# Putting a sparse graph layer's hand-ordered stage under the list scheduler, with a third early slot for 12 tiles and edge lists built in the message loop

## The chip, the cores and the metric

The kernel runs on one core of a Trainium2 chip. The metric is the device time of one execution in microseconds (us). Before the change three runs took 649.17, 649.49 and 644.71 us; their median, 649.17 us, is the time before.

## The reference

Four graph layers follow one another on the same 2708 nodes with 128 features. All use one sparse adjacency matrix `adj` (2708 x 2708; an entry is present with probability 0.003, so a row has some 8, and a row's present entries all have the value 1 divided by their number). Each layer adds to `x` a function of `h`, the rectified layer norm of `x`. `NORM`, `LOG`, `EXP` and `H_ADD` stand for the row norm, and for the hyperbolic logarithm, exponential and addition, each of which needs a few sums per row and a factor per row.

```python
# layer 0
h = max(layernorm(x), 0)
e = H_ADD(EXP(LOG(h) @ embed), embed_bias)
neigh = EXP(adj @ LOG(e))
x = x + H_ADD(EXP(LOG(concat(h, neigh)) @ layer), layer_bias)
# layer 1
h = max(layernorm(x), 0)
s, d = h @ msg_w[:, :D].T, h @ msg_w[:, D:].T
agg[i] = sum_j adj[i, j] * gelu(s[i] + d[j] + msg_b)
new = concat(h, agg) @ upd_w.T + upd_b
x = x + layernorm(gelu(new) + h) * ln_w + ln_b
# layer 2
h = max(layernorm(x), 0);  x = x + max(adj @ (h @ w2), 0)
# layer 3
h = max(layernorm(x), 0);  x = x + h @ w_self + (adj @ h / clip(rowsum(adj), 1)) @ w_neigh
```

The gelu of layer 1 stands inside the sum over edges, so the rows `d[j]` have to be fetched for every edge; the other layers use the matrix as a mask in plain products.

## The kernel before

**Tiling.** The nodes make T = 22 tiles of 128 rows (the last has 20 rows). Four tiles make a block, so there are six blocks, the last of two tiles. Blocks 0 to 2 (tiles 0 to 11) are the first half, blocks 3 to 5 (tiles 12 to 21) the second. The work of `sparse_stack` falls into a beginning, the sparse stage of layer 0, the message loop of layer 1, and layers 2 and 3. A flag that tells whether the matrix fits the kernel's lists is worked out beside it; if it is set, `dense_stack` computes everything again.

**The sparse stage of layer 0** (lines 818 to 1542) is written in order and lets the framework order the engines, apart from a few places where `queue_behind` holds an operation until another one has been issued.

- The rows of the embedding are scaled (line 1465) and cut into three bf16 parts (`split`, line 797). ACT and DVE turn the adjacency matrix, read by columns, into an fp8 mask (line 992). PE multiplies parts with mask, one product for each of the six blocks of columns (line 1284, 66 matmuls a block).
- For each block PE also packs the mask into words (line 1021). From these DVE finds which columns of a row are present (`find_words`, `find_columns`) and lays them out in slots (`lay_out`, `ext` at line 1130): two early slots, four head slots, and the rest of the edges in a tail of up to three lists of 128 edges a tile. `pack_edges` (line 1204) builds the tail's lists for a block of tiles: two DVE operations a tile (lines 1214 and 1217), three small matmuls a tile (line 1227), an ACT copy (line 1235) and some dozen DVE operations.
- `neighbours` (line 1316) and `update` (line 1357) finish layer 0 for one half: norms and factors, own rows (line 1342), new `x` (line 1368), normalised rows on ACT (line 920), their transposes on PE (line 930), the products `d` (line 941), and the writes of `d` to two tables in HBM: `d_hbm` for all nodes and `d_early` for the first half alone (line 1389). For the first half the transposes are held until three quarters of block 4's product have been issued.
- `gather_early` (line 1483) has POOL fetch the rows for the two early slots from `d_early`. This is 44 indirect DMAs of 128 rows. It can start when the first half's `d` is written, before the second half is finished. Columns of the second half that stand in an early slot are moved to the tail.

**The message loop of layer 1** (lines 1720 to 2195) is ordered by a list scheduler in the program itself. `op` records an operation with its engine, an assumed duration, what it follows and a due time; `carry_out` (line 1588) works through them in assumed time and issues them in that order, which then is the fixed order of each engine's queue. `ring` counts buffers: the operation waits until the one that many places earlier has been freed.

- `prelude` (line 1736) computes, for one block, the rows `s` and the rows' own part of the update, and cuts `s` into three parts.
- `messages` (line 1801) does one tile. POOL gathers the head slots and then the tail from `d_hbm`; both have four buffers. DVE adds `s`, ACT applies gelu, PE sums over the slots and multiplies by the update weights.
- `update` (line 1945) ends two tiles. `share` (line 2105) adds a tile's rows to the product of layer 2, and `check_half` (line 2136) compares the adjacency rows of 13 tiles with the found value in two halves of 1354 columns. Both are fillers, taken where an engine has nothing due.

```python
        g4 = op("POOL", 5.08, begin_head, gathered[-1:], when - 10.2, ring=("g", 4))
        g3 = op("POOL", 1.27 * nq, begin_tail, [g4], when - 5.1, ring=("gt", 4))
```

Each gather is one indirect DMA, so a full tile has seven in the loop, four for the head and three for the tail; all tiles together have 88 and 64. Layers 2 and 3 follow, ordered by the same scheduler; the change touches there only the sum over the checks' counts.

## Time and profile before

| what | before |
| --- | --- |
| median of the runs | 649.17 us |
| profiled execution, own time | 653.21 us |
| its span | 651.4 us |
| busy PE, DVE, ACT, POOL | 430.5, 412.4, 321.0, 224.0 us |
| gathers of the loop: head, tail | 88 of 1028 ns, 64 of 1008 ns |
| first product matmul (line 1284) | at 62.0 us |
| first and last early gather (line 1487) | at 169.4 and 226.2 us |
| first and last gather of the loop (line 1810) | at 272.8 and 511.3 us |
| last tile's new row in the loop (line 1890) | at 544.7 us |

The profile is of one execution. Times are counted from its first instruction; the span is from the first to the last one, and the execution's own time has a little around it. POOL is the engine that issues the gathers. [...] "Remote" or "another core or an unknown queue" as releaser of a wait means that the profile shows no event that ended it. Each engine works through its queue in order, so an operation that waits holds everything behind it.

### The profile page before, as it was taken

How to read it: one execution, taken by the hardware profiler on the slowest of the kernel's cores; microseconds unless marked ns; L12 is line 12 of the kernel's file. 1: busy time of each engine (PE TensorE's matmuls, PEld its weight loads, DVE VectorE, ACT ScalarE, POOL GpSimd, SP SyncE). 2: the span in 40 equal slices, each digit the busy share in tenths (PEclk: the TensorE clock that was granted, in tenths of full speed). 3: DMA queues.
4: the chain of work that ended last, by engine and by line, in shares of the span. 5: the costliest groups of instructions: out<-in, count | busy, mean ns of one | idle time of the engine just before them, and what ended most of it. 6: DMA issues, size and time to landing. Idle time of an engine off the chain costs nothing.

```text
span 651.4 us, 8164 instructions
## 1 busy us (share of the span) xinstructions
PE 430.5 (66%) x2467; PEld 295.6 (45%) x2467; DVE 412.4 (63%) x1715; ACT 321.0 (49%) x634; POOL 224.0 (34%) x277
## 2 busy tenths in 40 slices
PE   2956999999930003632177777837577888899875
PEld 2642444756720002532064544534445544678764
DVE  6879596578832166642155654565567648799963
ACT  3788677714200122321043533746567662899821
POOL 8500000000477700277465655665676300000000
PEclk9987999799955555666558987967799889999979
DMA  8884798200321100121131112665475240017502
GB/s 282 265 288 151 260 351 284 79 2 10 110 52 50 48 1 12 37 52 52 34 88 41 41 41 78 225 204 192 148 254 167 94 165 7 2 37 291 198 18 74
DMA packets 39363, 77.85 MB, mean 120 GB/s; under 512 B 5231, under 2 KB 18151, under 8 KB 38267
## 3 DMA queue, kind: packets, MB, share of 16 engines
q1 hardware_dynamic: 30846, 63.15, 28.3%
q0 software_dynamic: 6720, 13.38, 8.0%
q10 hardware_dynamic: 1744, 0.72, 0.4%
q8 instruction: 21, 0.34, 0.2%
q14 instruction: 32, 0.25, 0.1%
HBM read 73.62 MB, written 3.62 MB: 119 GB/s over the span
## 4 chain that ended last, share of the span: by engine, by line
PE 37%; DVE 25%; another core or an unknown queue 14%; ACT 13%; issue 5%; DMA 3%; POOL 2%; ACTq 0%; DVEq 0%
PE acc L1284 10%; PE two L2113 7%; DVE eq L2486 4%; ACT eq L2154 3%; PE pk L1021 2%; PE msg L1876 2%; PE three L2300 2%; ACT wm L1709 2%; PE msg L1870 2%; DMA layer_w<-in_L_gnn_layer_dram 2%; PE d L941 1%; POOL g L1810 1%; PE u L1424 1%; PE nd L1333 1%
## 5 line engine op out<-in xcount | busy, mean ns | idle before, releaser
L1810 POOL DMA_INDIRECT g<-d_hbm,head_c x88 | 90.5, 1028 | 106.1 <-DVE v L1751 45.7
L2113 PE MATMUL two<-mask,parts 128*128 128x512 fp8e4 (+1 forms) x288 | 71.1, 385 | 12.7 <-ACT parts L2044 5.7
L1810 POOL DMA_INDIRECT gt<-d_hbm,tail_c x64 | 64.5, 1008 | 24.1 <-issue 18.7
L1487 POOL DMA_INDIRECT early<-d_early,early_c x44 | 44.6, 1013 | 73.1 <-DMA d_hbm<-v 60.0
L2300 PE MATMUL three<-wm,pair 128*128 128x512 f32 (+1 forms) x264 | 62.9, 388 | 1.9 <-ACT pair L2359 1.8
L1284 PE MATMUL acc<-mask,parts 128*128 128x512 fp8e4 (+1 forms) x288 | 59.6, 358 | 0.6 <-DVE parts L802 0.4
L1709 ACT CAST wm<-mask 128x2708 fp32r<-128x2708 fp8e4 x22 | 53.3, 2450 | 7.1 <-DVE u L2064 7.0
L2300 PEld LDWEIGHTS three<-wm,pair 128*128 128x128 f32 x264 | 47.4, 194 | 11.7 <-ACT pair L2359 2.3
L2113 PEld LDWEIGHTS <-parts 128*128 128x128 bf16 x288 | 29.0, 106 | 40.1 <-issue 13.2
L930 PE MATMUL hTpm<-ident,h 128*128 128x128 f32 x22 | 5.1, 350 | 61.0 <-ACT h L920 61.0
L1876 PE MATMUL msg<-rt,gt 128*128 128x128 f32 x128 | 22.4, 318 | 33.5 <-ACT gt L1925 32.3
L1284 PEld LDWEIGHTS <-parts 128*128 128x128 bf16 x288 | 26.7, 99 | 37.8 <-ACT parts L799 7.5
L992 ACT ACTIVATE mask<-a 128x2048 fp8e4<-128x2048 uint32 (+3 forms) x27 | 37.9, 1433 | 9.0 <-DMA a<-in_adj_t_dram 9.0
L1021 PE MATMUL pk<-mask,shifts 128*128 128x512 fp8e4 (+1 forms) x132 | 31.6, 377 | 12.0 <-ACT mask L992 12.0
L1876 PEld LDWEIGHTS msg<-rt,gt 128*128 128x128 f32 x128 | 19.1, 219 | 39.4 <-ACT gt L1925 36.5
L2154 ACT ACTIVATE eq<-eq 128x1354 fp8e4<-128x1354 fp8e4 x26 | 34.4, 1326 | 4.9 <-DVE eq L2148 3.2
L1870 PE MATMUL msg<-ident,g 128*128 128x128 f32 (+1 forms) x176 | 28.3, 311 | 11.8 <-ACT g L1918 9.9
L1886 PE MATMUL msg<-upd_w,aggs 128*128 128x128 f32 x44 | 13.3, 394 | 30.6 <-issue 15.9
L1870 PEld LDWEIGHTS msg<-ident,g 128*128 128x128 f32 (+1 forms) x176 | 25.4, 219 | 16.5 <-ACT g L1918 12.4
L1859 DVE TENSOR_TENSOR gt<-gt,msg 128x384 f32<-128x384 f32 (+1 forms) x22 | 11.9, 540 | 31.4 <-remote 18.6
L930 PEld LDWEIGHTS hTpm<-ident,h 128*128 128x128 f32 x22 | 3.5, 173 | 62.1 <-ACT h L920 61.9
L2486 DVE TENSOR_SCALAR_CACHE_REDUCE eq<-row,val 128x1354 fp8e4<-128x1354 f32 (+1 forms) x18 | 29.2, 1620 | 0.3
(457 smaller groups left out, 1024.7 us busy)
## 6 DMA issues: line engine op xcount, KB each, us to landing
a<-in_adj_t_dram SPq DMA_DIRECT2D x25, 1024.0 KB
hT<-in_adj_dram SPq DMA_DIRECT2D x26, 677.0 KB
row<-in_adj_dram SPq DMA_DIRECT2D x8, 1354.0 KB
a<-in_adj_t_dram SPq DMA_DIRECT2D x5, 296.0 KB
g<-d_hbm,head_c POOLq DMA_INDIRECT x88
a<-in_adj_t_dram SPq DMA_DIRECT2D x5, 256.0 KB
d_hbm<-v SPq DMA_DIRECT2D x5, 256.0 KB
out_dram<-x SPq DMA_DIRECT2D x5, 256.0 KB
```

The costliest lines, as they stand in the source:

```text
L992: nc.scalar.activation(mask[:, g : g + n, sl], bits[:, :n, :w], AF.Sign, saturate=False)
L1021: nc.tensor.matmul(pk[:, :w], shifts[:, t, :], mask[:, t, sl], start=(t == 0), stop=(t == T - 1))
L1284: last = nc.tensor.matmul(acc[:, :w], part_of(t, k), mask[:, t, sl], start=(t == 0 and k == 0), stop=(t == T - 1 and k == 2),)
L1487: nc.gpsimd.indirect_dma_start(out=early_d[t // EACH][:n, t % EACH, k, :], out_offset=None, in_=d_early, in_offset=bass.IndirectOffsetOnAx ...
L1709: nc.scalar.copy(m, mask[:, t, :])
L1810: nc.gpsimd.indirect_dma_start(out=g[:n, q, :], out_offset=None, in_=d_hbm, in_offset=bass.IndirectOffsetOnAxis(ap=table[:n, q : q + 1], a ...
L1870: nc.tensor.matmul(sums(), box["g"][:n, q, :], ident[:n, :], start=False, stop=False)
L1876: nc.tensor.matmul(sums(), box["gt"][:, q, :], box["rt"][:, q, :], start=False, stop=(q == nq - 1),)
L2113: nc.tensor.matmul(two[b][:, : sl.stop - sl.start], part_of(t, k), mask[:, t, sl], start=(t == 0 and k == 0), stop=(t == T - 1 and k == 2),)
L2154: nc.scalar.activation(eq[0][:n, : c1 - c0], eq[0][:n, : c1 - c0], AF.Copy, accum_out=same[:n, t, k : k + 1], saturate=False,)
L2300: nc.tensor.matmul(three[b][:, : sl.stop - sl.start], made["pair"][:, t, k, :], wide_mask[t][:, sl], start=(t == 0 and k == 0), stop=(t == ...
L2486: nc.vector.tensor_scalar(eq[:n, : c1 - c0], my["row"][:n, c0:c1], val[:n, t : t + 1], None, op0=ALU.is_equal, op1=ALU.add, accum_out=same ...
```

## The change

The sparse stage of layer 0 is recorded with `op` and carried out by the list scheduler as well; the scheduler's functions move up, ahead of that stage. The order by hand and all `queue_behind` in the stage go. An operation without a due time is given one backwards from what follows it (`set_dues`), and the second call of `carry_out` continues from the times of the first. Six parts:

1. The products, the packing into words, the search, the layout and the ends of both halves are separate operations. A product's matmuls for a tile wait for this tile's parts and mask alone. The transposes of the first half no longer wait for block 4's product.
2. The first 12 tiles get a third early slot. Its 12 gathers come from `d_early` after the 44 others and land in `hT`, over the transposed rows of the first half, which therefore have to be used up first. The head of these tiles has three slots instead of four, so the loop gathers 12 rows' worth less from `d_hbm`: 76 for the head, 64 for the tail. A tile's third slot is added, put through gelu and summed by operations of its own.
3. The preludes of blocks 0 to 2 move into the first stage. There ACT copies the products, and the bias is added by a matmul with one row of ones instead of a DVE addition.
4. The edge lists of block 0 are built in the first stage and those of blocks 1 to 5 in the loop. The tail gathers of a tile, its positions and its edge sources wait for its block's list. The two DVE operations a tile become one absolute value on ACT and one comparison on DVE.
5. The loop's arrival times are worked out from the end of the first stage and the number of gathers of each tile, instead of a fixed period of 8.75.
6. The checks read thirds of 904 columns instead of halves of 1354, into four places instead of two (two in `hT`, two in the first buffer of early rows), 39 of them instead of 26.

```diff
-    def split(src, sl, left):
...
+    def set_dues(first):
+
+        latest = [400.0] * len(ops)
+        for i in range(len(ops) - 1, first - 1, -1):
+            o = ops[i]
+            if o["due"] is not None:
+                latest[i] = min(latest[i], o["due"])
+            else:
+                o["due"], o["auto"] = latest[i], True
+            for a, lag in o["after"]:
+                needed = latest[i] - between(ops[a]["engine"], o["engine"], lag)
+                latest[a] = min(latest[a], needed - ops[a]["took"])
...
+    def earlier(t):
+        return EARLY + 1 if t < first_half else EARLY
+
+    def third_of(t):
+        return hT[: rows(t), t * P : (t + 1) * P]
...
+            if bias is not None:
+                nc.tensor.matmul(
+                    by_tile[:, k, :], ones_row, bias[:1, :], start=False, stop=True
+                )
...
+        def distance(t):
+            box[t] = pool().tile([P, EDGES], F16, tag="apart", name=f"apart{t}")
+            nc.scalar.activation(box[t], edge_i, AF.Abs, bias=cen[:, t : t + 1])
+
+        def within(t):
+            nc.vector.tensor_scalar(
+                r_all[:, t, :], box[t], half_n[:, t : t + 1], None, op0=ALU.is_lt, saturate=False
+            )
...
+            a = op(
+                "ACT", 0.5, lambda t=t: distance(t), [*after, *packed[-1:]],
+                early(11.0 - 0.6 * (t - t0)), ring=("apart", 1),
+            )
+            r = op("DVE", 0.33, lambda t=t: within(t), [a], early(10.4 - 0.6 * (t - t0)))
...
+        w = op("PE", 0.0, begin, last, early(7.6), ring=one_ring)
+        p = op("PE", 0.2 * n, lambda: [columns(t) for t in range(t0, t1)], [w], early(7.5))
+        k = op("ACT", 0.45, take, [(p, 0.2), *packed[-1:]], early(6.0))
+        frees(w, k)
+        k = op("DVE", 1.25, choose, [k], early(5.0))
+        k = op("DVE", 1.7, pick, [k], early(3.5))
...
-        find_words(0, words_in(0), scaled)
-        sums = sums_of([0, 1, 2])
-        find_columns(groups[0])
-        product(0, sums)
...
-        formed = update([0, 1, 2], nc.scalar.copy, last)
...
-        gather_early(range(0, BLOCK))
...
-        for b in (0, 1, 2):
-            pack_edges(b, formed)
-        neighbours(late, sums)
-        update(late, nc.vector.tensor_copy, None)
-        for b in late:
-            pack_edges(b)
...
+        product_due = (5.5, 24.0, 43.5, 67.0, 86.0, 105.0)
+        words_due = (0, 19.0, 29.0, 62.0, 81.5, 100.5)
...
+        for t in range(T):
+            for k in range(EARLY):
+                e = op(
+                    "POOL", 1.265, lambda t=t, k=k: gather_early(t, k),
+                    [e, early_of[t], *((f, 2.3) for f in firsts)], due=99.0 + 1.265 * (2 * t + k),
+                )
+            early_op[t] = e
+        for t in range(first_half):
+            e = early_op[t] = op(
+                "POOL", 1.265, lambda t=t: gather_early(t, EARLY),
+                [e, *hT_reads, *(gone[b] for b in range(lead))], 165.0 + 1.265 * t,
+            )
+        gathered.append(e)
...
-        g4 = op("POOL", 5.08, begin_head, gathered[-1:], when - 10.2, ring=("g", 4))
-        g3 = op("POOL", 1.27 * nq, begin_tail, [g4], when - 5.1, ring=("gt", 4))
+        g4 = op("POOL", 1.265 * m, begin_head, gathered[-1:], when - 10.2, ring=("g", 4))
+        if t == 0:
+            ops[g4]["after"].extend((f, 2.4) for f in finals)
+        g3 = op("POOL", 1.265 * nq, begin_tail, [g4, packed_of[t // BLOCK]], when - 5.1,
+                ring=("gt", 4))
...
-    for g in range(len(groups)):
-        last_own = prelude(g, -4.0 + 3.0 * g if g < 2 else arrival[2 * g - 3] + 3.0)
...
+    for b in range(1, nb):
+        packed_edges(b, arrival[BLOCK * b] - 14.0, lambda: edges_p, ("one", 2), [])
...
+    for k in range(3 * CHECKS):
+        check_part(k // 3, k % 3, arrival[8] + 2.4 * k)
```

`firsts` and `finals` are the writes of `d` of the first and the second half, `hT_reads` the preludes' reads of the transposed rows, `m` the number of head slots of a tile.

## The prediction

> **What bounds the kernel now.** I first cut the span where the work changes character (edges from the timeline) and asked the windows view for each stretch: busy us of each engine with its instruction count, granted TensorE clock, DMA share, GB/s.
>
> ```profile
> 62.00:120.00 58.00, 57.29 (x291) 29.16 (x292) 39.45 (x195) 42.12 (x53) 0.19 (x1) 0.99 0.84 282
> 120.00:169.00 49.00, 48.75 (x281) 29.11 (x280) 42.72 (x232) 19.07 (x58) 0.00 (x0) 0.94 0.13 37
> 169.00:228.00 59.00, 13.77 (x127) 11.90 (x124) 19.40 (x89) 6.15 (x24) 44.59 (x44) 0.57 0.18 47
> 228.00:273.00 45.00, 12.17 (x75) 10.33 (x76) 28.14 (x142) 10.66 (x26) 0.19 (x1) 0.50 0.05 15
> 273.00:324.00 51.00, 14.24 (x91) 12.59 (x89) 16.58 (x41) 11.08 (x28) 34.61 (x36) 0.63 0.18 46
> 324.00:513.00 189.00, 134.47 (x814) 93.53 (x814) 113.03 (x389) 102.55 (x257) 120.20 (x117) 0.85 0.43 135
> 513.00:546.00 33.00, 26.55 (x147) 16.07 (x148) 22.03 (x105) 19.40 (x43) 0.00 (x0) 0.90 0.23 87
> 546.00:652.00 106.00, 87.55 (x470) 69.44 (x468) 81.36 (x264) 68.86 (x70) 0.00 (x0) 0.95 0.27 95
> ```
>
> The columns of busy time are PE, PEld, DVE, ACT, POOL. Up to 169 us PE is full. From 169 to 324 us, 155 us, no engine is full: first 44 gathers run and everything else falls nearly still, then the chain of the second half runs with POOL idle, then gathers again with everything else nearly still. From 324 us POOL's gathers pace the message loop; from 546 us the change touches almost nothing.
>
> The waits view says who stands still in those 155 us (total, times, longest):
>
> ```profile
> PE hTpm L930 <- ACT h L920: 61.0, 1, 61.0
> POOL early L1487 <- DMA d_hbm<-v: 60.0, 1, 60.0
> POOL g L1810 <- DVE v L1751: 45.7, 1, 45.7
> POOL g L1810 <- issue: 44.4, 75, 6.0
> ```
>
> PE idles 61 us for the second half's normalised rows; POOL idles 45.7 us between its last early gather and its first loop gather. The timeline shows why the chain behind PE's wait is slow: one gather every 1.25 us without a break, and a DVE row that needs only finished inputs.
>
> ```profile
> 223.73 0.94 POOL L1487 DMA_INDIRECT early<-d_early,early_c  x1 [0.30 <-issue]
> 224.15 1.13 DVE L1342 SCALAR_TENSOR_TENSOR h<-ne,n_kap,h 128x128 f32<-128x128 f32 x4 [10.95 <-remote]
> ...
> 226.19 0.90 POOL L1487 DMA_INDIRECT early<-d_early,early_c  x1 [0.31 <-issue]
> ...
> 233.25 0.61 DVE L1342 SCALAR_TENSOR_TENSOR h<-ne,n_kap,h 128x128 f32<-128x128 f32 x2 [7.97 <-remote]
> ...
> 316.49 0.95 POOL L1810 DMA_INDIRECT gt<-d_hbm,tail_c  x1 [0.30 <-issue]
> 322.76 0.55 DVE L1859 TENSOR_TENSOR gt<-gt,msg 128x384 f32<-128x384 f32 x1 [18.65 <-remote]
> ...
> 323.46 1.01 POOL L1810 DMA_INDIRECT g<-d_hbm,head_c  x1 [6.02 <-issue]
> ```
>
> In brackets stand idle time and releaser. Both times DVE moves again 5 to 6 us after the last gather of an unbroken string ended (227.1 to 233.25, 317.4 to 322.8). I read that as: during an unbroken string the other engines' signals arrive late. It is an inference from two places; the waiting chain costs little work.
>
> **What the Trainium skill says.** "SBUF — State Buffer", section "SBUF: two separate sides", says some DVE operations lock GpSimd out while it writes descriptors. The trace agrees: a gather takes 0.95 us in quiet stretches and up to 1.75 us (at 405 us) beside busy DVE. It also says PE and ACT wait on nobody there; the trace differs for whatever reason, ACT at L1883 waiting up to 10.3 us for matmuls that had ended. "Perfetto Trace Analysis", section "DMA Instruction — SWDGE (GPSIMD)", says the recorded end is the end of descriptor writing, not of the transfer; here the chain of waits shows 2.3 to 3.1 us from a gather to its landing. "TensorE: Matmul & The Clock Gate", Part 1, says an idle array drops to half clock: 0.50 granted from 228 to 273 us.
>
> **The change, part by part.** The sum is against the profiled execution: span 651.4 us, its own time 653.2, against a median of 649.17 of the runs shown; I subtract the same saving from the median.
>
> *Earlier start of the products, −5.* The first product matmul is at 62.0 us although the first rows (L1465) are scaled at 51.7. In the new order each tile's matmuls wait for their own group: four rows of 0.28 and a three-part split, 4 to 5 us. PE's work after that is unchanged, so the last product ends near 168 instead of 173.
>
> *The first half's hand-over, −10 more.* Its factor chain runs from 119.5 (L1320) to 143.8 (L914); relu starts at 148.9 behind other ACT work, and the transposes are held until 158.05 behind three quarters of product 4. Unheld, 143.8+13 (relu to last write, 148.9 to 166.4 less 4.5 held)=157, plus landing, less the 5 us: early gathers start at about 154 instead of 169.4.
>
> *POOL's string.* 44 early gathers took 57.7 us (169.4 to 227.1): 154+58=212. The new thirds are 12 gathers at 1.31: 228. The loop's first gather queues behind them, so POOL alone allows 228, against 272.8 before. This is the best end.
>
> *The second half's chain.* It began at 178.4 (L1320) and ended its last table write near 264.4: 86 us, of which 48.7 beside the string. The same chain for the first half needed 24.3+13=37 us. From 173, unhindered: 173+37+3=213, under POOL's 228. Hindered as before, it gets through only to the ninth own row, then needs 31 us (233.25 to 264.4): 212+6+31+3=252 if the string stops at the 44th gather, 267 if the thirds follow without a break. What speaks for something between is that the string can now break: gathers of tiles 12 to 21 wait for the second half's lists, the thirds for the preludes' matmuls, and until 181 us, while DVE had work of its own, DVE ran on beside the gathers. I take 243, close to the middle of 228 and 267. That is −30.
>
> *Moved out of the way.* The edge lists of five blocks cost DVE 4×0.31+4×0.61+3.3, about 7 us each before. After, the interval test is one ACT absolute value (no such row; its nearest are ACT copies, 0.3 to 0.5) and one 0.31 compare, so DVE pays 4.5 per block, ACT 2.4, in the loop. There DVE is busy 113 of 189 us and ACT 103, so 22 and 12 us fit into idle time; that cover ends if they stand in front of a gather (rival 3). Preludes of three blocks move ahead of the loop; additional bias matmuls, a K=1 product each, have no row: between zero, under PE's 61 us idle, and 12 tiles×2×0.5=12 us at half clock. I take zero.
>
> *Thirds in the loop, −16.* POOL spent 155.0 busy and 60.4+24.1 idle on 152 gathers after its first: busy and the usual 0.30 between them make 1.32 each. Twelve fewer save 15.8. Each of the 12 tiles gets one more DVE add (nearest row 0.42, for two slots) and one more ACT gelu (0.4), against a shorter head add (0.69 for four): hidden with the rest. Matmul count stays.
>
> *Opening of the loop, −6, block boundaries, +5.* Before, 35 gathers run until 317.4 and tile 1 is finished only then. After, the ring of four buffers holds 24, and 12 tiles' preludes are done: I take 6 of the 11×1.3=14 us. Five times a tail gather waits for an edge list; where the list is early this is zero, with one broken handoff of the kind above 10; I take 1 each.
>
> *Nothing.* 39 checks of 904 columns for 26 of 1354: same elements, 13 more starts at 0.1 to 0.2 on DVE and ACT as filler, 13 more loads on SP, a queue that issues little else in the loop; SP's reads of adjacency stand ahead of table writes, but all landed by 125 us. One more add for the third count: 0.2 us.
>
> Sum: 243−272.8=−30, −16−6+5=−17, together −47. Span 604, own time 606, median 602.
>
> **The rivals.** (1) *POOL is the bound throughout.* Late signals are avoided: loop at 228 (−45), loop −22, and of the 33 us after the last gather (512 to 546) a dozen go, since edge lists keep POOL less far ahead: −79, 570. For it: 1.25 us gathers leave engines free by occupancy; against: the two stretches of stillness. (2) *The string moves and so does the stillness.* Loop at 267 (−6), loop −16, boundaries +5: −17, 632. For it: same gathers, same chain, still overlapping. (3) *Slower: the edge list becomes POOL's wait.* A tail gather of tile 4b now waits for ACT, DVE, PE, ACT, DVE, DVE in turn, queued in order behind consumers that run four tiles late; all later gathers of POOL queue behind it. With one handoff held for 10.3 to 18.6 us at each of five boundaries this costs 50 to 90; at 70 with −52 otherwise it gives 667. It decides from 52/5=10.4 per boundary; slower by 1% from 11.7. Against it: a waiting POOL ends its string, which frees the signals. (4) *No effect.* A smaller hold, 8 to 11 at each boundary, eats the gain: 643 to 656.
>
> **Chances.** About 1% (6.5 us) is what a measurement can tell here. The forecast's case, 588 to 620: 0.43; rival 1: 0.22; rival 2, with values up to 642.7: 0.14; within 1%: 0.07; slower: 0.14. Faster is thus 0.79. The range from 557 to 652 leaves out slower ends and some 0.05 below. My own case alone is 588 to 620.
>
> **What would show it.** Right: first early gather near 154, 12 gathers more before the loop, PE's wait for L920's successor far under 61, first loop gather near 243, 140 gathers in the loop. The mechanism is wrong if DVE and ACT work on normally beside an unbroken string, or stay late when POOL is idle. The forecast fails if POOL's tail gathers wait on edge lists longer than 10 us, if the second half's chain ends after 260, or if the last loop row still comes 270 us after the loop's first gather.

## The result and the profile after

Four runs of the changed kernel took 668.07 to 669.45 us, median 668.53; four of the kernel before on the same chip 644.71 to 649.49, median 648.10. The ratio is 1.0325 (95% interval 1.028 to 1.037): the change makes the kernel 3% slower. The profiled execution has an own time of 668.64 us and a span of 666.8, against 653.21 and 651.4 before. The one before is 5 us longer than its median, so the spans differ by 15.4 us where the medians differ by 20.4.

The windows view of the kernel after, cut at its own edges (first early gather at 161.24, loop's gathers from 267.69 to 535.7; 219 only parts the stretch between them). Columns of busy time are PE, PEld, DVE, ACT, POOL, then granted clock, DMA share, GB/s:

```profile
161.00:219.00 58.00, 31.69 (x183) 23.90 (x180) 23.23 (x102) 8.39 (x24) 33.66 (x36) 0.62 0.16 40
219.00:268.00 49.00, 34.78 (x127) 24.67 (x126) 29.66 (x149) 16.18 (x44) 21.09 (x22) 0.50 0.15 40
268.00:536.00 268.00, 153.35 (x944) 108.53 (x945) 143.89 (x540) 128.75 (x348) 137.27 (x140) 0.74 0.34 101
536.00:667.00 131.00, 107.69 (x578) 81.89 (x576) 97.96 (x338) 82.10 (x99) 0.00 (x0) 0.94 0.28 99
```

Two things are to be seen. Between 161 and 268 us, taken as a whole, still no engine is full, although the stretch starts 8 us earlier than before. And the loop's gathers now last 268 us with 137 us of POOL's work in them; before, 152 gathers with 155 us of work lasted 239.5. The 15.4 us between the spans are therefore: loop's first gather −5.1 (267.7 for 272.8), loop +28.5, what follows the last gather −8.0 (131.1 for 139.1).

The waits view of the kernel after says what POOL stood for (total, times, longest):

```profile
POOL g L2296 <- issue: 43.2, 68, 9.5
...
POOL gt L2296 <- DVE rx L909: 20.8, 1, 20.8
...
POOL gt L2296 <- PE two L2614: 17.8, 2, 17.5
POOL g L2296 <- DVE lefts L1028: 15.4, 1, 15.4
...
POOL gt L2296 <- DVE eq L2656: 12.7, 1, 12.7
POOL gt L2296 <- PE msg L2357: 12.4, 1, 12.4
```

Four tail gathers wait 12.4 to 20.8 us, together 63.4. They are the first tails of tiles 8, 12, 16 and 20, at 354.8, 404.5, 471.7 and 525.6 us. The releasers that the view names are whatever ended last by the profile's reckoning and are all different. The timeline says what was really late, here for block 2 (tiles 8 to 11):

```profile
315.67 0.42 DVE L1081 TENSOR_SCALAR r_all<-apart,n_half 128x384 fp8e4<-128x384 f16 x1
...
335.93 0.83 PE L2361 MATMUL msg<-ident,g 128*128 128x128 f32 x6
...
344.19 0.49 PE L2377 MATMUL msg<-upd_w,aggs 128*128 128x128 f32 x2 [1.62 <-ACT aggs L2374]
...
346.64 0.83 PE L2361 MATMUL msg<-ident,g 128*128 128x128 f32 x6
347.31 0.46 PE L1087 MATMUL ex<-edge_x,r_all 128*128 128x27 f16 x12
...
350.47 0.42 ACT L1097 COPY exs<-ex 128x324 f32<-128x324 f32 x1
...
353.83 0.17 DVE L1132 TENSOR_SCALAR tail_c<-cf 128x12 uint32<-128x12 f32 x1
...
354.84 0.94 POOL L2296 DMA_INDIRECT gt<-d_hbm,tail_c  x1 [12.41 <-PE msg L2357]
```

The last interval test ends at 316.1. The twelve small matmuls that need it (0.46 us) run at 347.3, directly behind the head sums of a tile at 346.64. Counted from the loop's start these are the sixth head sums, tile 5's. The list's PE work thus stands in PE's queue behind tile 5, and ACT and DVE take 6 us more; POOL, which may run four tiles ahead (tile 4's sums at 335.93 freed the buffer for tile 8's head), needs it four tiles ahead. Block 1's list was ready at 299.8, before its gather at 302.3, and cost nothing.

The other finding is in the timeline before the loop, here of PE, ACT and DVE:

```profile
166.98 0.27 PE L1587 MATMUL wp<-ident,wt 128*128 128x128 f32 x1 [0.34 <-issue]
...
195.29 0.37 ACT L1593 CAST wt<-wp 128x256 int32<-128x256 f32 x1 [27.16 <-remote]
195.70 0.43 DVE L1624 SCALAR_TENSOR_TENSOR wt<-wt,place 128x256 int32<-128x256 int32 x1 [26.97 <-ACT wt L1593]
...
231.05 0.17 DVE L2037 SCALAR_TENSOR_TENSOR n_s<-n_s,n_z 128x10 f32<-128x10 f32 x1 [1.23 <-DVE n_s L2037]
232.45 0.17 DVE L2037 SCALAR_TENSOR_TENSOR n_s<-n_s,n_z 128x10 f32<-128x10 f32 x1 [1.23 <-DVE n_s L2037]
233.85 0.17 DVE L2037 SCALAR_TENSOR_TENSOR n_s<-n_s,n_z 128x10 f32<-128x10 f32 x1 [1.23 <-DVE n_s L2037]
...
238.98 0.17 DVE L2052 TENSOR_TENSOR n_s<-n_s,n_f 128x10 f32<-128x10 f32 x1
```

DVE waits 27 us for an ACT operation that itself waited 27.2 us, although the PE operation whose result it copies had ended at 167.3. POOL issues a gather every 1.25 us meanwhile, until 191.0; ACT goes on 4.3 us later. The last product on PE stands still as well: it ended at 172.7 before and ends at 196.5 here. Around 231 each step of a chain of dependent DVE operations waits 1.23 us for the DVE operation ahead of it, 1.40 us a step for 0.17 us of work, again beside gathers every 1.25 us. These gathers pause at 234.3; from 238.1 on the long waits are gone, and DVE is busy for 27 of the next 30 us. Each engine seems to hear of finished work about once a gather. This is the stillness of the profile before, seen on single steps.

### The profile page after: what moved, and what is told of

Same layout as the page of the kernel before. It is cut to its first block, busy times and chain, and to the rows that moved or that the text cites. A ratio compares the mean times of both kernels' runs of the same rounds, so it can differ in the third digit from the quotient of the medians.

```text
span 666.8 us, 8385 instructions
## 1 busy us (share of the span) xinstructions
PE 459.4 (69%) x2515; PEld 314.4 (47%) x2515; DVE 422.8 (63%) x1725; ACT 337.4 (51%) x700; POOL 216.6 (32%) x275
## 4 chain that ended last, share of the span: by engine, by line
PE 34%; DVE 27%; another core or an unknown queue 14%; ACT 11%; issue 9%; DMA 3%; ACTq 0%; POOL 0%; DVEq 0%
PE acc L1871 11%; PE two L2614 7%; DVE eq L3002 3%; PE pk L1571 3%; PE three L2816 2%; ACT wm L2261 2%; PE msg L2367 2%; DMA layer_w<-in_L_gnn_layer_dram 1%; DVE n_s L2037 1%; DMA row<-in_adj_dram 1%; ACT eq L2662 1%; PE msg L2361 1%; PE u L1429 1%; DVE eq L2656 1%
## 5 line engine op out<-in xcount | busy, mean ns | idle before, releaser
L2296 POOL DMA_INDIRECT g<-d_hbm,head_c x76 | 75.1, 989 | 60.8 <-issue 43.2
L2178 POOL DMA_INDIRECT early<-d_early,early_c x44 | 41.5, 944 | 161.2 <-DMA d_hbm<-v 134.7
L2296 POOL DMA_INDIRECT gt<-d_hbm,tail_c x64 | 62.4, 976 | 85.1 <-DVE rx L909 20.8
L1871 PE MATMUL acc<-mask,parts 128*128 128x512 fp8e4 (+1 forms) x288 | 63.1, 366 | 19.5 <-ACT parts L1546 9.1
L1871 PEld LDWEIGHTS <-parts 128*128 128x128 bf16 x288 | 27.3, 101 | 51.7 <-issue 12.6
L1508 ACT ACTIVATE mask<-a 128x2048 fp8e4<-128x2048 uint32 (+5 forms) x29 | 34.8, 1232 | 11.2 <-DMA a<-in_adj_t_dram 11.2
L2662 ACT ACTIVATE eq<-eq 128x904 fp8e4<-128x904 fp8e4 (+1 forms) x39 | 36.8, 944 | 0.8 <-DVE eq L2656 0.7
L1871 PE MATMUL acc<-mask,partsh 128*128 128x512 fp8e4 (+1 forms) x108 | 24.4, 366 | 13.7 <-issue 13.7
L2427 ACT ACTIVATE gt<-gt 128x384 f32<-128x384 f32 (+1 forms) x22 | 11.2, 508 | 41.8 <-DVE gt L2348 30.1
L2381 DVE SCALAR_TENSOR_TENSOR u<-msg,val,tmp 128x128 f32<-128x128 f32 x22 | 7.6, 347 | 36.6 <-remote 28.8
L2377 PE MATMUL msg<-upd_w,aggs 128*128 128x128 f32 x44 | 11.9, 359 | 26.8 <-issue 24.9
L2614 PE MATMUL two<-mask,partsh 128*128 128x512 fp8e4 (+1 forms) x108 | 24.2, 378 | 6.5 <-ACT partsh L2543 4.2
L2361 PE MATMUL msg<-ident,g 128*128 128x128 f32 (+1 forms) x152 | 25.7, 318 | 2.8 <-issue 2.3
```

The costliest lines, as they stand in the source:

```text
L1508: nc.scalar.activation(to, patterns, AF.Sign, saturate=False)
L1871: nc.tensor.matmul(box["acc"][:, :w], part_of(t, k), mask[:, t, sl], start=(t == 0 and k == 0), stop=(t == T - 1 and k == 2),)
L2178: nc.gpsimd.indirect_dma_start(out=to, out_offset=None, in_=d_early, in_offset=bass.IndirectOffsetOnAxis(ap=early_c[:n, t, k : k + 1], axi ...
L2296: nc.gpsimd.indirect_dma_start(out=g[:n, q, :], out_offset=None, in_=d_hbm, in_offset=bass.IndirectOffsetOnAxis(ap=table[:n, q : q + 1], a ...
L2361: nc.tensor.matmul(sums(), box["g"][:n, q, :], ident[:n, :], start=False, stop=False)
L2614: nc.tensor.matmul(two[b][:, : sl.stop - sl.start], part_of(t, k), mask[:, t, sl], start=(t == 0 and k == 0), stop=(t == T - 1 and k == 2),)
```

## The experiments

Two causes are in question. **Theory A**: the list waits are real lost time. **Theory C**: gathers without a break hold the signals between the other engines. The table gives, for each run, the start of the loop's first gather, from there to the end of the last one ("loop"), the rest of the span, the median, and the ratio to the kernel before on the same chip (95% interval; its median lay between 643.1 and 648.5 there). The first three columns are from the profiled execution. Two executions can differ by some 8 us there: e7 is the kernel before in all but some copies that change nothing, and has 264.6 and 234.4 where before has 272.8 and 239.5. The medians of runs on different chips are compared by their ratios.

| run | first gather | loop | rest | median | ratio to before |
| --- | --- | --- | --- | --- | --- |
| before | 272.8 | 239.5 | 139.1 | 648.10 | |
| after | 267.7 | 268.0 | 131.1 | 668.53 | 1.033 (1.028–1.037) |
| e1 lists in first stage | 294.5 | 223.0 | 137.6 | 655.34 | 1.017 (1.008–1.026) |
| e2 lists due 54 ahead | 267.5 | 221.9 | 139.4 | 632.12 | 0.984 (0.976–0.991) |
| e12 lists due 29 ahead | 266.2 | 224.1 | 140.8 | 632.16 | 0.982 (0.975–0.989) |
| e3 breaks of 4 | 264.6 | 258.2 | 131.7 | 652.68 | 1.014 (1.005–1.022) |
| e4 early rows by SP | 230.5 | 257.4 | 128.6 | 619.04 | 0.963 (0.954–0.971) |
| e5 lists 54, breaks of 4 | 263.6 | 223.6 | 140.1 | 631.98 | 0.980 (0.973–0.986) |
| e6 lists 54, breaks of 8 | 249.8 | 223.1 | 143.3 | 619.18 | 0.957 (0.951–0.964) |
| e8 lists 54, tiny operation | 267.9 | 226.3 | 142.0 | 637.50 | 0.983 (0.977–0.990) |
| e9 lists 54, no third | 280.1 | 237.7 | 140.6 | 662.70 | 1.033 (1.024–1.042) |
| e10 e6 and breaks in loop | 249.0 | 222.3 | 141.6 | 616.79 | 0.960 (0.953–0.967) |
| e15 lists 29, breaks of 8, no third | 238.7 | 240.2 | 138.8 | 620.01 | 0.964 (0.957–0.971) |
| e7 before, copies without a pause | 264.6 | 234.4 | 140.2 | 649.54 | 1.000 (0.997–1.003) |
| e11 before, breaks of 8 | 241.1 | 232.8 | 140.4 | 613.54 | 0.952 (0.945–0.958) |
| e13 before, busy breaks of 8 | 241.9 | 234.6 | 136.3 | 615.47 | 0.957 (0.950–0.963) |
| e14 before, breaks of 16 | 243.0 | 233.1 | 137.1 | 618.41 | 0.960 (0.954–0.966) |

### When the edge lists are built (e1, e2, e12)

e1 records all lists in the first stage; e2 and e12 leave them in the loop and only move their due times.

```diff
-        packed_edges(0, 190.0, lambda: small, ("one0", 4), [tailed[0]])
+        for b in range(nb):
+            packed_edges(b, 190.0 + 8.0 * b, lambda: small, ("one0", 4), [tailed[blocks[b][0]]])
...
-    for b in range(1, nb):
-        packed_edges(b, arrival[BLOCK * b] - 14.0, lambda: edges_p, ("one", 2), [])
```

> The kernel after the change, with the edge lists of blocks 1 to 5 also recorded in the first stage beside that of block 0; nothing is left out. Theory A (rival 3: the tail gathers of tiles 8, 12, 16 and 20 stand waiting for lists that are queued behind consumers on PE, ACT and DVE, 63.5 us in all): the four waits vanish, the loop's first gather stays within 5 us of 267.7, its last comes some 30 to 50 us earlier than 534.7, own time 620 to 640. Theory B (the consumers of gathered rows set the pace of the loop, and a wait for a list only takes the place of a wait for a buffer): the pauses move to the head gathers, the last gather comes less than 15 us earlier, own time 652 to 668.

```diff
-        packed_edges(b, arrival[BLOCK * b] - 14.0, lambda: edges_p, ("one", 2), [])
+        packed_edges(b, arrival[BLOCK * b] - 54.0, lambda: edges_p, ("one", 2), [])
```

> The kernel after the change, with the due time of each list in the loop 54 us before its block's first tile instead of 14; nothing is left out. It asks whether the place in the loop or only the place in the queue matters. Theory A: a list that stands in the queues more than four tiles ahead is early enough, the waits of 12 to 21 us at tiles 8, 12, 16, 20 fall under 3 us each, own time 620 to 645, near the run that builds all lists in the first stage. Theory B: 652 to 668, pauses moved to the head gathers.

e12 has 29.0 in that place.

> The kernel after the change with the lists due 29 us ahead of their block, which is two tiles of the loop more than 14. POOL runs up to four tiles ahead of the consumers behind which the lists stand in the queues. Theory A, priced by distance: two more tiles halve the four waits, to some 4 to 9 us each, own time 640 to 655; if already two tiles free them, 630 to 637; if only a full lead of four tiles helps, 660 to 669.

In e1 and e2 the four list waits are gone, in e12 all but one of 5.8 us (tile 16, whose list ends at 432.5 and whose tail starts at 433.3), and the loop is 44 to 46 us shorter: theory A holds, and theory B (a buffer wait takes their place) falls. Of the 63.4 us, 46 come back in the loop; the rest turns into other, shorter waits. By the medians, each against the kernel before on its own chip, the late lists cost 32 us: 20.4 slower with them, 11.4 faster in e2. e2's waits view of POOL has what is left:

```profile
POOL g L2296 <- issue: 27.3, 58, 3.4
POOL gt L2296 <- issue: 17.9, 57, 0.8
POOL g L2296 <- DVE parts L1037: 13.5, 1, 13.5
```

The 13.5 us precede the loop's first gather; no tail gather waits more than 2.1 us. e12 shows where the point lies: 15 us more lead bring as much as 40. In the plan a tile of six gathers lasts 7.5 us and one of seven 8.75, so 14 us are less than two tiles and 29 between three and four, just short of the four that POOL's buffers let it run ahead.

e1's first half failed: the loop started 27 us late, at 294.5 instead of within 5 us of 267.7. The last operation of the last list ends at 293.7 on DVE, 0.8 us before the first gather. In e1 the lists of blocks 1 to 5 come out one after another behind that of block 0, which ends at 259.1, some 7 us each, with little beside them; those of blocks 3 to 5 can't be built before the second half's layout. (That the gather waits for them because the loop's buffers lie where the first stage's were is likely, and was not isolated.) Built where the waits are short but nothing hides them, the lists cost most of what they save: 27 us at the start and 6.5 after the last gather, for 45 in the loop.

### What the string of gathers does (e3, e4, e8)

e3 makes POOL wait after each fourth early gather for its rows to land; e4 takes the string off POOL. Its plain loads bring other rows than those of the edges, so the early part of the sums is left wrong.

```diff
             nc.gpsimd.indirect_dma_start(
                 out=to,
...
             )
+            taken_in.append(to)
+            if len(taken_in) % 4 == 0:
+                landed = small.tile([1, 1], F32, tag="landed", name=f"landed{len(taken_in)}")
+                nc.gpsimd.tensor_copy(landed, to[:1, :1])
```

> The kernel after the change; after each fourth of the 56 early gathers POOL copies one element of the rows just gathered, so it must wait for them to land, some 2 to 3 us; nothing is left out. Theory C (while gathers follow one another every 1.25 us, signals between other engines pass only once in a gather or less; chains of dependent DVE operations that need 0.2 us a step take 1.25 to 1.4): DVE's idle stretch of 27 us from 168.7 to 195.7 shrinks under 10, the steps at 227 to 238 take 0.2 to 0.4, the second half's chain (last operation before the loop's first gather) ends before 240 instead of 262 to 267; the string itself grows by 14 x 2.5 = 35 us, so the first loop gather stays between 255 and 285. Rival D (the chain is slow by its own clock or its own order): the idle stretch stays over 20 us and the loop's first gather comes at 285 or later.

```diff
-            nc.gpsimd.indirect_dma_start(
-                out=to,
-                out_offset=None,
-                in_=d_early,
-                in_offset=bass.IndirectOffsetOnAxis(ap=early_c[:n, t, k : k + 1], axis=0),
-            )
+            nc.sync.dma_start(out=to, in_=d_early[:n, :])
```

> The kernel after the change; the 56 early gathers on POOL become plain loads of the same size on SP's queue, that take the first rows of the table instead of those of the edges, so the early part of the sums over edges is left wrong and its time counts as that of the transfers alone. Theory C: with no string on POOL the second half's chain runs as the first half's did, the loop's first gather comes at 215 to 235, own time 615 to 640 (with the list waits kept). Rival D: the chain ends at 255 or later as before, own time 655 to 668.

The same two places of DVE's timeline in e3:

```profile
167.96 0.42 DVE L1081 TENSOR_SCALAR r_all<-apart,n_half 128x384 fp8e4<-128x384 f16 x1 [0.68 <-ACT apart L1078]
168.29 0.42 DVE L1624 SCALAR_TENSOR_TENSOR wt<-wt,place 128x256 int32<-128x256 int32 x1
...
189.82 0.17 DVE L2035 TENSOR_SCALAR n_s<-n_z 128x10 f32<-128x10 f32 x1
190.02 1.40 DVE L2037 SCALAR_TENSOR_TENSOR n_s<-n_s,n_z 128x10 f32<-128x10 f32 x7
```

The operation at 195.70 now runs at 168.29 without a wait, and seven steps of L2037 take 1.40 us together, 0.20 each, where one took 1.40. The last product on PE ends at 169.5 instead of 196.5. The second half's last table write, which the loop's first gather needs, is issued at 225.6 us instead of 264.5, much as in e4 with no gathers at all (227.7). So theory C holds, and four gathers in a row hold nothing that can be seen. In e4 the loop starts at 230.5, and the ratio falls from 1.033 to 0.963, some 45 us. In e3 the chain is ready as early, but POOL itself, with 14 pauses of some 2 us, is done only at 264: of the gain 3 us are in the start and 10 in the loop; why the loop is shorter was not looked into.

e5 joins e2 and e3; e6 has half as many breaks; e8 puts a tiny operation between all early gathers that waits for nothing:

```diff
-            if len(taken_in) % 4 == 0:
+            if len(taken_in) % 1 == 0:
...
-                nc.gpsimd.tensor_copy(landed, to[:1, :1])
+                nc.gpsimd.memset(landed, 0.0)
```

> Both edits at once on the kernel after the change: lists due 54 us ahead, and a copy of one landed element after each fourth early gather. If the list waits and the hold by the string are two separate causes, the gains add: the loop's first gather at 265 as with the breaks alone, 221 us of gathers as with the earlier lists alone, end near 620, own time 612 to 626. If one hides the other (the loop catches up later with what the start gains), own time stays at 628 to 636.

> As e5, but a break after each eighth early gather: 7 breaks instead of 14, which saves POOL about 13 us. Theory C1 (what counts is how long a run of gathers lasts, and runs of 8, about 10 us, are short enough): the second half's chain still ends before 240, the loop's first gather comes at 246 to 254, own time 600 to 612. Theory C2 (the hold begins within the first eight gathers): DVE stands still for more than 3 us several times between 165 and 240, the chain ends at 245 to 262, own time 612 to 632.

> As e5, but instead of waiting for landed rows POOL writes one element after every early gather, a short operation that waits for nothing. Theory P (any end of a gather run, however short, lets the held signals pass): the chain ends before 240, the loop's first gather comes at 245 to 255. Theory Q (POOL must stand idle, or its transfers must have landed, for the signals to pass): the chain ends at 258 to 275 as without breaks, first loop gather at 265 or later, own time 628 to 645.

e5 missed: 632.0, no better than the lists alone. POOL's string, 56 gathers and 14 pauses, ends at 262.7 and sets the start by itself. e6, with runs of 8, lies between its two theories: DVE stands still longer than 3 us three times (5.3, 4.2, 3.8), the last table write is issued at 239.8, POOL is done at 248.9 and the loop starts at 249.8, as theory C1 has it, but the time is 619.2 us. e8 decides against theory P: the last table write is at 264.8. These are POOL's timeline of e8 and, below, DVE's:

```profile
206.14 0.94 POOL L2180 DMA_INDIRECT early<-d_early,early_c  x1 [0.23 <-issue]
207.08 0.09 POOL L2189 MEMSET landed<- 1x1 f32 x1
207.39 0.95 POOL L2180 DMA_INDIRECT early<-d_early,early_c  x1 [0.21 <-issue]
```

```profile
233.93 0.17 DVE L2037 SCALAR_TENSOR_TENSOR n_s<-n_s,n_z 128x10 f32<-128x10 f32 x1 [1.17 <-DVE n_s L2037]
235.32 0.17 DVE L2037 SCALAR_TENSOR_TENSOR n_s<-n_s,n_z 128x10 f32<-128x10 f32 x1 [1.23 <-DVE n_s L2037]
```

The operation of 0.09 us fits into the 0.30 us that lie between two gathers anyway: the gathers stay 1.25 us apart, and the steps at 1.4 us. So another POOL operation between the gathers is not enough; a break has to last. How long, and doing what, is asked below.

### The kernel before, with breaks (e7, e11, e13, e14)

The string is in the kernel before, too, so its gathers get the same breaks and nothing else is changed. Up to the loop's first gather DVE, ACT and PE run the same operations in the same order as before in all four runs, so a changed order is no rival here.

> The kernel before the change with the same breaks after each fourth of its 44 early gathers and nothing else. If the string held the second half's chain there too (48.7 of its 86 us lay beside the string): the loop's first gather comes at 244 to 258 instead of 272.8, and 10 to 25 us are saved, own time 622 to 638. If the stillness there has another cause (order by hand, PE at half clock): the first loop gather stays at 268 or later and the time within 1% of before.

e7 had the copy of e3 with no order to the gathers behind it, and the framework issued each copy a group later, when its rows had long landed. No gather was put off, and the ratio is 1.000: copies between the gathers do nothing by themselves. (The profiled execution is a quick one, 641.0 us for a median of 649.5, so its first gather at 264.6 says little.) In e11 each group is issued behind the copy:

```diff
-                    nc.gpsimd.indirect_dma_start(
...
+                    with queue_behind(hold[0]):
+                        nc.gpsimd.indirect_dma_start(
...
+                    taken_in.append(early_d[t // EACH][:1, t % EACH, k, :1])
+                    if len(taken_in) % 8 == 0:
+                        landed = small.tile([1, 1], F32, tag="landed", name=f"landed{len(taken_in)}")
+                        hold[0] = nc.gpsimd.tensor_copy(landed, taken_in[-1])
```

> The kernel before the change with a break after each eighth of its 44 early gathers; in the former try of this (e7) the framework issued the copies one group later, so that POOL did not pause at all, and nothing changed. Here each group of gathers is issued after the copy of the group before. If unbroken runs hold the second half's chain here too: POOL pauses 1.5 us five times, DVE's long idle stretches there (10.5, 11.0, 8.0 us) fall under 6, the loop's first gather comes at 242 to 262 instead of 272.8, own time 622 to 640. If not: within 1% of before.

POOL's timeline of e11 at the first break, and DVE's beside it:

```profile
183.30 0.95 POOL L1490 DMA_INDIRECT early<-d_early,early_c  x1 [0.30 <-issue]
185.85 0.18 POOL L1501 COPY landed<-early 1x1 f32<-1x1 f32 x1 [1.60 <-DMA early<-d_early,early_c]
186.19 0.98 POOL L1490 DMA_INDIRECT early<-d_early,early_c  x1 [0.16 <-issue]
```

```profile
192.28 0.17 DVE L1328 TENSOR_TENSOR n_nsq<-n_th,n_hsq 128x10 f32<-128x10 f32 x1
192.36 0.34 DVE L1342 SCALAR_TENSOR_TENSOR h<-ne,n_kap,h 128x128 f32<-128x128 f32 x1
192.70 2.41 DVE L1342 SCALAR_TENSOR_TENSOR h<-ne,n_kap,h 128x128 f32<-128x128 f32 x9
```

All ten own rows run in one piece by 195.1; before, the last two of them ran at 233.25 (the prediction shows that line). DVE's stretches of 10.5, 11.0 and 8.0 us are gone; up to the last table write, at 224.8 instead of 264.7, its longest is 3.0 us, a wait for PE's transposes. The loop starts at 241.1, which is POOL's own end, and the median is 613.5: five pauses, 1.9 to 2.6 us from the end of one gather to the start of the next (some 1.6 of them the wait for the rows), save 4.8%. It has the lowest median and ratio of all runs.

In e13 POOL waits for nothing in its breaks but works 2.5 us on something else; in e14 there are only two breaks, after 16 and 32 gathers.

```diff
-                        nc.gpsimd.indirect_dma_start(
+                        latest_gather = nc.gpsimd.indirect_dma_start(
...
-                        hold[0] = nc.gpsimd.tensor_copy(landed, taken_in[-1])
+                        with queue_behind(latest_gather):
+                            for _ in range(4):
+                                work = small.tile([P, P], BF16, tag="work", name=f"work{len(taken_in)}")
+                                hold[0] = nc.gpsimd.tensor_scalar_mul(work, ident, 1.0)
```

> The kernel before the change, as e11, but in each of its five breaks POOL waits for nothing: it runs four element-wise operations of 128x128 (0.54 us each in the trace of before, together some 2.2 us) between two groups of eight gathers. Theory R (a break of some 2 us without gathers is enough, landed or not): as e11, first loop gather at 241 to 250, own time 612 to 624. Theory S (the gathers issued must have landed before more follow): DVE's long idle stretches stay, first loop gather at 262 or later, own time within 1.5% of before.

> The kernel before the change with a break after each sixteenth of the 44 early gathers, two breaks in all. If the hold begins only after some 8 gathers and its length grows with the run, the result lies between e11 (241.1, 613.5) and before (272.8, 648): first loop gather at 248 to 262, own time 622 to 638. If two breaks are as good as five: 613 to 620. If runs of 16 hold as much as 44: 640 or more.

```profile
181.52 0.95 POOL L1490 DMA_INDIRECT early<-d_early,early_c  x1 [0.30 <-issue]
182.51 2.50 POOL L1503 TENSOR_SCALAR work<-ident 128x128 bf16<-128x128 f32 x4
185.16 1.01 POOL L1490 DMA_INDIRECT early<-d_early,early_c  x1 [0.16 <-issue]
```

This is e13's first break on POOL's timeline: gathers that follow 2.5 us of other work, with no wait for rows. It is as good as e11 (615.5, the intervals overlap), so theory R holds: what is needed is that no gather is issued for 2 to 3 us (2.6 to 2.8 in e13), not that rows have landed, nor that POOL stands idle. e14 falls into its second case, two breaks nearly as good as five: 618.4, the first gather only 2 us later than in e11, though DVE again has stretches of 6.2 and 8.5 us. What sets the start there is no longer POOL, whose string ends at 232.6; DVE's edge lists, the last of which ends at 242.2, are the likely cause.

### The third slot (e9, e15) and breaks in the loop (e10)

e9 is e2, and e15 is e12 with breaks of 8, each with the third slot undone:

```diff
     def earlier(t):
-        return EARLY + 1 if t < first_half else EARLY
+        return EARLY
...
-        for t in range(first_half):
-            e = early_op[t] = op(
-                "POOL", 1.265, lambda t=t: gather_early(t, EARLY),
...
-            if t < first_half:
+            if earlier(t) > EARLY:
```

> The kernel after the change with the lists due 54 us ahead and without the third early slot: 44 early gathers, 88 head gathers and 64 tail gathers in the loop, as before the change. It prices the third slot by itself, against the run with earlier lists (267.5 first loop gather, 220.9 to the last, own time 632.1). The prediction's terms: without the 12 thirds the string ends 15 us sooner and the second half's chain comes free then, so the loop's first gather is at about 252; the loop's 12 gathers more cost 15.8, so it takes 237; together within 5 us of 632. Rival: the chain does not gain from the shorter string, first gather at 262 or later, own time 640 to 648.

> The kernel after the change with lists due 29 us ahead, a break after each eighth early gather, and no third early slot. Against e6 (third slot kept: first loop gather 249.8, 222.1 us to the last, own time 619.2): 12 gathers and two breaks fewer let POOL be ready at 231, but the second half's chain ends near 236 to 242, so the loop starts some 8 to 14 us earlier and lasts 15.4 us longer: own time 619 to 628. If the thirds are free beside the chain, it is 630 or more.

In the loop the 12 gathers cost what was expected, 15.8 us (237.7 for 221.9). The start of e9 was the surprise: later, not earlier. With the order that comes out there, POOL's 44 gathers run from 161.4 to 216.9 without one pause over 1 us, and DVE's layout of the second half crawls beside them; these are lines of its timeline, all of them steps that took 0.2 us each in e3:

```profile
204.45 0.20 DVE L1757 TENSOR_SCALAR reale<-ext 128x80 f32<-128x80 f32 x1 [7.42 <-remote]
...
212.85 0.17 DVE L1762 TENSOR_TENSOR n_nm<-n_nw,n_nm 128x10 f32<-128x10 f32 x1 [1.23 <-DVE n_nm L1761]
214.26 0.17 DVE L1763 TENSOR_TENSOR deg<-n_nm,n_ne 128x10 f32<-128x10 f32 x1 [1.24 <-DVE n_nm L1762]
```

In e2 POOL had to pause 8.6 us for that layout, at 201.4; in e9 the layout's first part was done before POOL needed it, and no pause came. An accident of order thus seems to have moved the start by 12.6 us (it was not isolated further), and e9 is 30 us slower than e2. With breaks (e15 for e6) the start moves 11.1 us forward, the loop grows by 17.1, and 620.0 for 619.2 is no difference that the intervals (0.957–0.971 and 0.951–0.964) can tell: within that the third slot takes from the loop what it adds to the string. The two runs differ in the lead of the lists, too: in e15, with 29 us, tile 12's tail still waits 8.3 us for its list.

e10 adds a break after the last tail gather of each of tiles 0 to 4 to e6.

> The kernel of e6 (lists 54 us ahead, a break after each eighth early gather, own time 619.2) with a break after the last tail gather of each of the first five tiles too. Theory C says the hold acts in the loop's opening as well, where some 24 gathers follow one another: the consumers of tiles 0 to 4 then begin within 6 us of their rows, the buffers come free sooner, and the 8 us wait near tile 10 and the other ring waits shrink by more than the 5 x 1.9 us that the breaks cost: own time 608 to 617. If the opening's stillness is repaid by POOL's lead anyway: 618 to 628.

The median, 616.8, is at the edge of its first case, but the loop lasts 222.3 us for 223.1, and the intervals of the two runs (0.953–0.967, 0.951–0.964) tell no difference. The wait of 8 us is gone, others of 4.9 and 6.9 took its place, and DVE still stood 18.9 us once before the add of a tail. Whether more breaks in the loop would bring anything stays open.

## Why the prediction was wrong

It said 602 and faster; the median is 668.5. By its own terms:

- **"Earlier start of the products, −5", "hand-over, −10 more".** The first early gather was to come at 154 instead of 169.4 and came at 161.2, 8.2 of the 15 us. The products start no earlier: the first product matmul is at 55.3 and was at 54.8 before. The 62.0 us of the prediction and of the table of before is not the first one, but where a long run of them begins. POOL's start mattered little, because the second half's chain set the loop's start. What the text left out is that a string that starts earlier also holds the last product: it ended at 196.5 and not at 168 (169.5 in e3, with breaks).
- **"I take 243 … That is −30": mis-sized, +25.** The mechanism, late signals during an unbroken string, was right, and e3, e11 and e13 show it. The choice of a value between 228 and 267 was not. The first gather came at 267.7. The breaks that the text counted on were there (13.7 us at 204.8, 5.4 at 239.7), but DVE had by then stood still for 27 us, from 168.7, after only six gathers; the layout that POOL then waited for was itself what the string held. The estimate of 213 for an unhindered chain was too early as well: e4, with no string, starts at 230.5, because from the end of the last product (172.2) to the last table write (227.7) it takes 55 us, not 37.
- **"Block boundaries … I take 1 each": the step that failed, about +38.** Measured: four waits of 12.4 to 20.8 us, 46 us of loop (268.0 for e2's 221.9), less 8 us after the last gather, where a late POOL leaves less to do (131.1 for e2's 139.4); 38.0 in the span, 32 by the medians. The reason given against rival 3, that a waiting POOL frees the signals, missed the point: the list's matmuls had a place in PE's queue behind consumers that run four tiles after POOL, and there they wait whether POOL is still or not. (The loop's opening stood still again beside 30 gathers, PE for 27.2 us up to 311.3, and that put the consumers back. But e2 has the same opening, PE idle for 24.9 us up to 309.8, and none of the four waits.) The price was in the profile before: POOL's head start is its ring of four, and the diff gives the list 14 us, less than two tiles of the plan.
- **"Thirds in the loop, −16", "opening, −6".** With the lists early enough the loop takes 221.9 instead of 239.5, −17.6 against the −22 of the two terms. The thirds alone are 15.8 (e9), as forecast. Whether the opening gave 2 us or 6 or nothing can't be told: e7, which is nearly the kernel before, has a loop of 234.4 for before's 239.5.
- **"Nothing" for checks, bias matmuls and the rest.** e2 leaves 139.4 us after the loop's last gather for 139.1 before. These terms hold within what is seen; they weren't tried singly.

Summed: −47 forecast, +25 for the start, some 0 for loop and rest, +38 for the lists, gives +16; measured +15.4 in the span. The parts of this sum are from single executions, and that of before was a long one; by the medians the change costs 20.4 us and the lists alone 32, so all else gained 11.

**Rival 3** gave 667, and with the right wait at the right place, but its two parts erred against each other: 70 for the lists where 32 to 38 were lost, −52 for all else where −11 (e2's median) to −23 (its span) was gained. **Rival 2**'s 267 for the start came out, in part by luck: it was worked out for a string that ends at 228 and 40 us of recovery and chain behind it. In fact the chain came free at 238.1, in a pause of POOL, and took 29.6 us from there, while the string went on to 252.2. The two rivals belonged together, each was taken as a case by itself, and the case in which both come true had no number: rival 2 without its own 5 for the boundaries is 627, and with the 38 measured afterwards 665. The chance of 0.14 for slower was too low, for the same text noted that rival 3 decides at 10.4 us a boundary.

Two smaller readings were off and cost nothing. The longest gather before took 2.65 us (at 169.4), not 1.75. And "the trace differs" sets ACT's 10.3 us, a wait for a finished operation, against a statement on SBUF's ports; no run here shows a wait for a port.

## What to carry to other kernels

When an engine runs ahead of its consumers by a ring of buffers, whatever it needs to go on must stand in every queue ahead of those consumers, by at least the depth of the ring; a due time of less than that ahead of the first use is too late (at 14 us four waits of 12.4 to 20.8 us; at 29 us one of 5.8 in e12 and one of 8.3 in e15; at 54 us none in e2, and one at tile 4, of 3.7 to 7.8, in e5, e6 and e8). When one engine issues indirect gathers in a long row beside a chain of small dependent steps, look at the steps on the other engines: if each waits about one period of the gathers (here 1.23 us beside gathers every 1.25), try a pause of 2 to 3 us after every eight gathers, and make sure in the profile that it is a pause. And where the profile before shows a hold, price it from the case without luck; don't take the middle between luck and none.

## What was not expected of the hardware

- Dependent DVE operations of 0.17 us that take 0.20 us a step in e3 take 1.40 us a step beside an unbroken string of gathers at 1.25 us, each waiting for the DVE operation ahead of it: the hold isn't limited to signals from one engine to another.
- It reaches every engine that depends on others: beside the first 24 gathers of the kernel after ACT stood for 27.2 us with its input ready, and PE's last product ended 27 us later than in e3.
- It begins within a run: six gathers (7.5 us) passed in the kernel after before DVE stood still; groups of four showed none of it, groups of eight nothing over 3.0 us in e11 but up to 5.3 us in e6.
- A pause of 1.9 to 2.6 us, from the end of one gather to the start of the next, in which POOL waits for rows and one of 2.6 to 2.8 us in which it computes end the hold alike (613.5 and 615.5). An operation of 0.09 us after each gather, which leaves the usual 0.30 us between gathers, doesn't (ratio 0.983 with it, 0.984 without). Pauses between 0.3 and 1.9 us were not tried, and what in the chip holds the signals stays open.
